# Three edits of order in a two-layer gated cross-attention kernel: when the router spreads its scores, when heads are transposed, when integers are transposed

## The chip, the cores and the metric

The kernel runs on one core of one Trainium2 chip. The metric is the device time in microseconds (us) of one execution; the median of several runs is compared. The core's engines run side by side, each through its own queue in order: TensorE (PE in the profile, with its weight loads as PEld), VectorE (DVE), ScalarE (ACT), GpSimd (POOL), and SyncE (SP), which here only issues transfers.

## The reference

Two layers act on x, which is 2 batches of 2048 tokens by 512 numbers. Each layer is a cross-attention to a context of 128 tokens and a feed-forward part, both gated:

```python
x = x + tanh(g_xattn[0]) * L0_xattn(layernorm(x), ctx_768, ...)
x = x + tanh(g_ffn[0])   * L0_ffn(layernorm(x), ...)
x = x + tanh(g_xattn[1]) * L1_xattn(layernorm(x), ctx_768, ...)
x = x + tanh(g_ffn[1])   * L1_ffn(layernorm(x), ...)
```

`L0_xattn` has 16 heads of 32 numbers, `L1_xattn` 16 heads of 64. `L0_ffn` is a mixture of depths: it works on 256 chosen tokens of each batch and leaves the others as they are.

```python
scores = x @ w_router
_, idx = top_k(scores, 256)
x_sel = take_along_axis(x, idx)
...                                   # causal self-attention and a gated MLP on x_sel
out = x.at[idx].set(x_proc)
```

`L1_ffn` multiplies by weights of -1, 0 and 1 with inputs rounded to integers in -128 to 127 (one scale per token), convolves over three neighbouring tokens, applies silu, rounds again and multiplies again.

## The kernel before

**Tiling.** Tokens go in 32 tiles of 128 rows; four tiles make a block of 512 tokens, four blocks a batch, so eight blocks in all, numbered 0 to 7. Matmuls in the attentions are in float32.

**Stages.** The first attention with the router (about 30 to 560 us of the profiled execution), the selected tokens' attention and MLP (560 to 830), the second attention with the first half of the integer feed-forward part beside it (830 to 1640), and the second half of that part (1640 to the end).

**Units.** `cross_attention` (L213) is called once for each layer. Its main loop (L338) steps through units: unit U is head u = U mod 16 of block n = U div 16. A unit issues, in this order:

- `scores` (L263) for the heads that share a tile of queries (four heads at once in the first layer, two in the second), and for its own head `probabilities` (L280): the softmax of `softmax_rows` (L113), which is a maximum `nmx` on DVE, four exps on ACT, a reciprocal `rden` on DVE, and the scaling of the tile A on POOL;
- at u == `ahead` (8 in the first layer, 10 in the second), `front` (L229) of the next block: layer norm on DVE, transposes `ptr` on PE, copies on ACT; and every fourth unit the next `queries` (projection `pq` on PE);
- `transposed` (L286) for the head two units back: four transposes `tp` on PE and a DVE copy to AT;
- `values` (L292), once in four units, for four heads of which the last is four units back: matmuls `po` on PE and ACT copies to OT;
- one step of `back` (L307), the output projection `pp` of an earlier block, which has eight steps and ends in a DVE addition to `x`;
- `beside(u)`, which advances other work.

A lies in a ring of four tiles, AT in a ring of six. In PSUM, `tp`, `po`, the router's `pb` and the gather's `pi` share two buffers (tag `o`).

**The router.** When `back` of block n ends, `router(n)` (L442) is appended to a list. `beside` (L436) takes two pieces of the list per unit. The pieces of a router are: the statistics; four rows (one for each tile: normalise on DVE, write it out through SP, multiply by `w_router` and sum with `ws` on DVE, scale `x` on ACT, write it out through SP); and then the work of `ranks` (L483). That begins with `spread` (L497), in which four transposes `pb` on PE broadcast the block's 512 scores over all partitions and an ACT copy puts them in `sb`. After it come counts on DVE (`junk`, L492, and `jd`, L514), which count for each token how many of its batch have a larger score: four tiles are new in each block, and the 4 x blk older ones of the batch are counted against the new scores, so the work grows with the block's number blk in its batch. After the last block of a batch, `gather` (L531) turns ranks to indices with 16 one-hot tiles `oh` on DVE and 32 small matmuls `pi` on PE, and two indirect transfers from POOL fetch the chosen rows.

With `back` of block n starting at unit 16n+19 and ending at 16n+26, the pieces start at unit 16n+26, and the spread comes in unit 16n+28, the same as the last row.

**The integers.** In the second attention, `quantize_rows` (L957) is a generator in a list `stream`, of which `beside4` takes two pieces per unit, and later one piece per third of an output tile. Its pieces are statistics, four tiles of scaling and maximum, four tiles of rounding to integers `xi` (ACT and then DVE, L980), then four steps of transposes `pt` on PE with an ACT copy to `xiT` each (L986 and L987), and the broadcast `inv_b`. The generator `first_half` of the same block follows in the same list; its matmuls `ph` (L1002) read `xiT`.

**Order.** The code's order gives each instruction its place, but an engine's queue in the trace isn't in that order word for word: instructions of different pieces are interleaved when the program is built. It is fixed from then on, and each engine waits for the instruction at its head.

Of the kernel before, what the change touches and what calls it, by code (L numbers as in the profile page):

```python
# [10 lines left out]
F32 = mybir.dt.float32  # L11
# [32 lines left out]
def flamingo_kernel(ctx: ExitStack, tc: tile.TileContext, a: dict, out: bass.AP):  # L44
# [167 lines left out]

    def cross_attention(  # L213
        W, act, hold, ps_mm, ps_sc, ps_o, row, xnT_bufs, ahead, rows_of, after_block, beside,
        after_units=lambda: None,
    ):

        L, nE, bias = W.L, W.nE, W.bias
        E = nE * P
        dh = E // H
        hpc = P // dh
        cpg = 4 // hpc
        scale = 1.0 / math.sqrt(dh)

        def front(n):  # L229

            tiles, xn, residual = rows_of(n)
            mv, rstd = ln_stats(tiles, L + "ln")
            for i, t in enumerate(tiles):
                normalize(xn[i], t, mv, rstd, i)
            xnT = act.tile([P, DC, BLK], F32, name="xnT", tag="xnT", bufs=xnT_bufs)
            transpose_block(
                ps_mm, "mm", xn, lambda d, pt: nc.scalar.copy(xnT[:, d, :], pt)  # L237
            )
            return residual, xnT

        def queries(xnT, grp):

            qT = [act.tile([P, BLK], F32, name="qT", tag="qT", bufs=3) for _ in range(cpg)]
            for c in range(cpg):
                e = grp * cpg + c
                pq = ps_mm.tile([P, BLK], F32, name="pq", tag="mm")
                for d in range(DC):
                    nc.tensor.matmul(  # L248
                        pq,
                        W.wq[:, d, ts(e, P)],  # L250
                        xnT[:, d, :],
                        start=(d == 0),
                        stop=(d == DC - 1),
                    )
                if bias:
                    nc.vector.tensor_scalar(
                        qT[c], pq, W.bq[:, e : e + 1], scale, ALU.add, ALU.mult
                    )
                else:
                    nc.scalar.activation(qT[c], pq, AF.Copy, scale=scale)  # L260
            return qT

        def scores(b, qT, e):  # L263

            sc = [ps_sc.tile([P, TB, M], F32, name="sc", tag="sc") for _ in range(hpc)]
            for t in range(TB):
                for h in range(hpc):
                    r = slice(h * dh, (h + 1) * dh)  # L270
                    nc.tensor.matmul(  # L271
                        sc[h][:, t, :],
                        qT[e % cpg][r, ts(t, P)],
                        W.kT[r, b, e, :],
                        start=True,
                        stop=True,
                    )
            return sc

        def probabilities(sc):  # L280

            A = act.tile([P, TB, M], F32, name="A", tag="A", bufs=4)
            softmax_rows(sc, TB, M, act, row, A)
            return A

        def transposed(A, AT):  # L286
            tp = ps_o.tile([P, TB, P], F32, name="tp", tag="o")
            for t in range(TB):
                nc.tensor.transpose(tp[:, t, :], A[:, t, :], ident)  # L289
            nc.vector.tensor_copy(AT, tp.rearrange("p t n -> p (t n)"))  # L290

        def values(b, AT, OT, grp):  # L292
            for c in range(cpg):
                po = ps_o.tile([P, BLK], F32, name="po", tag="o")
                for h in range(hpc):
                    hd = grp * 4 + c * hpc + h
                    nc.tensor.matmul(  # L297
                        po[h * dh : (h + 1) * dh, :],
                        W.v[:, b, ts(hd, dh)],
                        AT[c * hpc + h],  # L300
                        start=True,
                        stop=True,
                    )
                OT.append(hold.tile([P, BLK], F32, name="OT", tag="OT", bufs=nE + cpg))
                nc.scalar.copy(OT[-1], po)  # L305

        def back(n, residual, OT):  # L307

            tiles = residual()
            for t in tiles:  # L310
                nc.gpsimd.tensor_tensor(t, t, W.bo, ALU.add)  # L311
            for i, t in enumerate(tiles):
                pp = ps_mm.tile([P, D], F32, name="pp", tag="mm")
                for e in range(nE):
                    nc.tensor.matmul(  # L315
                        pp,
                        OT[e][:, ts(i, P)],
                        W.wo[:, e, :],
                        start=(e == 0),
                        stop=(e == nE - 1),  # L320
                    )
                    if e == nE // 2 - 1:
                        yield
                nc.vector.scalar_tensor_tensor(t, pp, W.g, t, ALU.mult, ALU.add)  # L324
                if i == TB - 1:
                    after_block(n, tiles)
                yield

        N = B * NBLK
        residual, xnT = {}, {}
        residual[0], xnT[0] = front(0)
        next_qT = queries(xnT[0], 0)
        As, AT, OT, out_of = {}, {}, {}, iter(())
        for U in range(N * H + 12):  # L338
            n, u = divmod(U, H)
            if n < N:  # L340
                grp, t = divmod(u, 4)
                if t == 0:
                    qT = next_qT
                if u % hpc == 0:
                    sc = scores(n // NBLK, qT, u // hpc)
                As[U] = probabilities(sc[u % hpc])
                if u == ahead and n + 1 < N:
                    residual[n + 1], xnT[n + 1] = front(n + 1)
                if t == 1 and grp < 3:
                    next_qT = queries(xnT[n], grp + 1)  # L350
                elif t == 1 and n + 1 < N:
                    next_qT = queries(xnT[n + 1], 0)
            V = U - 2
            if 0 <= V < N * H:
                AT[V] = act.tile([P, BLK], F32, name="AT", tag="AT", bufs=6)
                transposed(As.pop(V), AT[V])
            V = U - 4
            if 0 <= V < N * H and V % 4 == 3:
                n, grp = divmod(V // 4, 4)
                if grp == 0:  # L360
                    OT[n] = []
                values(n // NBLK, [AT.pop(i) for i in range(V - 3, V + 1)], OT[n], grp)
                if grp == 3:
                    out_of = back(n, residual.pop(n), OT.pop(n))
                    if n == N - 1:
                        after_units()
            next(out_of, None)
            beside(u)
# [23 lines left out]
    with ExitStack() as st:  # L392
# [49 lines left out]
        def router(n, tiles):  # L442
# [13 lines left out]
            for i in range(TB):  # L456
                t = t0 + i
                xn = act.tile([P, D], F32, name="xn2", tag="xn2", bufs=2)
                normalize(xn, x[t], mv, rstd, i)
                nc.sync.dma_start(out=xn_d[b][ts(t - b * TPB, P), :], in_=xn)  # L460
                ws = act.tile([P, D], F32, name="ws2", tag="ws2", bufs=1)
                nc.vector.scalar_tensor_tensor(
                    ws, xn, 1.0, w_router, ALU.mult, ALU.mult,
                    accum_out=score[:, t : t + 1],
                )
                nc.scalar.activation(
                    x[t],
                    x[t],
                    AF.Identity,
                    scale=keep_mul[:, i : i + 1],  # L470
                    bias=keep_add[:, i : i + 1],
                )
                nc.sync.dma_start(out=x_d[b][ts(t - b * TPB, P), :], in_=x[t])
                yield
            for work in ranks(b, blk):
                work()
                yield
# [102 lines left out]
        def stage1_rows(n):  # L580
# [3 lines left out]

        cross_attention(
            W0, act, act, ps_mm, ps_sc, ps_o, row, 2, 8, stage1_rows,
            lambda n, tiles: pending.append(router(n, tiles)), beside,
        )
        while pending:
            beside(None)  # L590
# [366 lines left out]
    def quantize_rows(g, tiles):  # L957
# [19 lines left out]
        for i, o in enumerate(tiles):  # L977
            nc.scalar.activation(o, o, AF.Copy, scale=s[:, i : i + 1], bias=RND)
            q = act4.tile([P, D], BF16, name="xi4", tag="xi4", bufs=TB)
            nc.vector.tensor_scalar(q, o, RND, 127.0, ALU.subtract, ALU.min)  # L980
            xi.append(q)
            yield
        for d in range(DC):
            pt = ps_mm.tile([P, BLK], BF16, name="pt4", tag="mm")
            for i, q in enumerate(xi):
# [373 lines left out]
```

## Time and profile before

| | us |
|---|---|
| median of 3 runs | 1854.61 (1854.43 to 1861.38) |
| the profiled execution | 1854.16 |
| its span, first to last instruction | 1852.5 |
| TensorE, weight loads, VectorE, ScalarE, GpSimd busy | 1660.6, 832.8, 1311.2, 1050.8, 527.4 |
| TensorE busy in 30 to 560 (first attention, router) | 440.2 of 530 |
| in 560 to 690 (selected attention) | 106.8 of 130 |
| in 690 to 880 (selected MLP, keys and values) | 181.3 of 190 |
| in 880 to 1640 (second attention) | 733.4 of 760 |
| in 1640 to the end (second half) | 182.7 of 213 |

Busy times overlap, since the engines work side by side. TensorE's granted clock is given as a share of full speed; its mean over the execution was 0.951. A line of the waits names the engine and line that stood, what it waited for, and the total, the number of times and the longest of these waits. In a timeline a line gives start, duration, engine, source line and operation, with the idle time before it in brackets.

### The profile page before, as it was taken

The numbers are of one execution on the slowest core, as the hardware profiler recorded it, in microseconds if no ns is written. First come the engines' busy times: TensorE is split into PE (matmuls) and PEld (weight loads), VectorE is DVE, ScalarE is ACT, GpSimd is POOL, SyncE is SP. The second block draws the span as 40 slices with busy tenths as digits, with TensorE's granted clock in tenths as the row PEclk, the third lists the DMA queues.
The fourth block names the chain that finished last, engine by engine and source line by source line (L and its number), as shares of the span: only waits on it lengthen the run. The fifth ranks groups of instructions, "written<-read, shape, count | busy, mean of one in ns | idle before, by whom it ended". The sixth has DMA issues, their size and how long they took to land.

```text
span 1852.5 us, 24500 instructions
## 1 busy us (share of the span) xinstructions
PE 1660.6 (90%) x7706; PEld 832.8 (45%) x7706; DVE 1311.2 (71%) x2769; ACT 1050.8 (57%) x3065; POOL 527.4 (28%) x666
## 2 busy tenths in 40 slices
PE   6989988888836989989999999999999999898969
PEld 3544544444413444445544454444444454443423
DVE  5777897887783642224537779889888888876966
ACT  2745544354501535304537778878787787754556
POOL 4534434342300320032214333322423243220200
PEclk9999999899967889999999999999999999998989
DMA  7011011011144009330011233334133133155465
GB/s 287 1 46 47 1 47 46 12 46 47 46 139 156 1 9 314 112 91 23 26 35 55 97 114 105 128 120 154 52 135 127 77 109 123 74 203 205 150 229 191
DMA packets 98456, 184.36 MB, mean 100 GB/s; under 512 B 11327, under 2 KB 30527, under 8 KB 94614
## 3 DMA queue, kind: packets, MB, share of 16 engines
q1 hardware_dynamic: 97430, 180.70, 28.1%
q0 software_dynamic: 896, 2.10, 0.6%
q8 instruction: 61, 1.00, 0.2%
q14 instruction: 69, 0.57, 0.1%
HBM read 108.31 MB, written 74.45 MB: 99 GB/s over the span
## 4 chain that ended last, share of the span: by engine, by line
PE 34%; DVE 14%; DMA 6%; ACT 5%; issue 2%; POOL 2%; SPq 1%; POOLq 0%; DVEq 0%; ACTq 0%
PE pp L315 8%; PE pq L248 7%; DVE h L1018 3%; PE ph L1002 3%; PE sc L271 2%; PE po L297 2%; PE pu L875 2%; PE pw L875 2%; PE acc L861 2%; PE tp L289 2%; PE po L1231 1%; DMA hf<-h_d 1%; DMA x<-h_d 1%; DVE u L1012 1%; DMA hq<-hq_d 1%
## 5 line engine op out<-in xcount | busy, mean ns | idle before, releaser
L119 ACT ACTIVATE A<-sc,nmx 128x128 f32<-128x128 f32 x1024 | 362.9, 377 | 171.7 <-DVE nmx L116 149.8
L128 POOL TENSOR_TENSOR A<-A,rden 128x512 f32<-128x512 f32 x256 | 274.4, 1073 | 479.9 <-DVE rden L127 373.1
L315 PE MATMUL pp<-L_wo,OT 128*128 128x512 f32 x768 | 365.9, 610 | 12.7 <-DVE x L324 4.7
L248 PE MATMUL pq<-xnT,L_wq 128*128 128x512 f32 x768 | 358.0, 612 | 0.2 <-ACT xnT L237 0.2
L119 ACT ACTIVATION_READ_ACCUMULATOR A<-sc,nmx 128x1 f32 x1024 | 221.4, 216 | 0.0
L248 PEld LDWEIGHTS pq<-xnT,L_wq 128*128 128x128 f32 x768 | 145.7, 197 | 159.6 <-issue 151.7
L116 DVE TENSOR_REDUCE nmx<-sc 128x4 f32<-128x512 f32 x256 | 169.2, 678 | 66.6 <-PE sc L271 66.5
L290 DVE COPY AT<-tp 128x512 f32<-128x512 f32 x256 | 172.8, 677 | 55.5 <-PE tp L289 55.1
L315 PEld LDWEIGHTS pp<-L_wo,OT 128*128 128x128 f32 x768 | 139.0, 195 | 159.6 <-issue 134.9
L1018 DVE SCALAR_TENSOR_TENSOR h<-u,cw,h 128x512 f32<-128x512 f32 x256 | 191.4, 782 | 5.6 <-ACT h L1014 5.1
L289 PE MATMUL tp<-ident,A 128*128 128x128 f32 x1024 | 164.3, 282 | 28.7 <-POOL A L128 26.6
L271 PE MATMUL sc<-L_kT,qT 32*128 32x128 f32 (+1 forms) x2048 | 164.0, 291 | 8.1 <-ACT A L119 5.1
L271 PEld LDWEIGHTS sc<-L_kT,qT 32*128 32x128 f32 (+1 forms) x2048 | 130.8, 189 | 87.2 <-issue 59.3
L289 PEld LDWEIGHTS tp<-ident,A 128*128 128x128 f32 x1024 | 119.3, 143 | 103.9 <-issue 48.0
L1231 PE MATMUL po<-w2q,hq 128*128 128x512 bf16 x512 | 121.2, 392 | 18.2 <-DVE hq L1213 8.5
L1014 ACT ACTIVATE h<-u,cb,cw 128x512 f32<-128x512 f32 x128 | 99.2, 809 | 64.7 <-DVE u L1012 60.1
L1002 PE MATMUL ph<-xiT,w1q 128*128 128x512 bf16 x512 | 125.1, 381 | 2.6 <-DVE u L1012 2.3
L297 PE MATMUL po<-AT,L_v 128*32 128x512 f32 (+1 forms) x512 | 115.9, 623 | 7.9 <-DVE AT L290 7.5
L305 ACT COPY OT<-po 128x512 f32<-128x512 f32 x96 | 55.7, 588 | 101.4 <-PE po L297 100.9
L1012 DVE TENSOR_TENSOR u<-ph,inv_b 128x512 f32<-128x512 f32 x128 | 85.1, 683 | 31.8 <-PE ph L1002 26.9
L1011 POOL COPY u<-carry 128x2 f32<-128x2 f32 x128 | 49.2, 386 | 192.0 <-DVE h L1018 159.6
L311 POOL TENSOR_TENSOR x<-x,L_bo 128x512 f32<-128x512 f32 x64 | 87.3, 1382 | 33.8 <-DMA x<-x_d 14.3
(216 smaller groups left out, 2203.3 us busy)
## 6 DMA issues: line engine op xcount, KB each, us to landing
h_d<-h SPq DMA_DIRECT2D x28, 1024.0 KB, 3.9
x_d<-x SPq DMA_DIRECT2D x64, 256.0 KB, 2.5
hf<-h_d SPq DMA_DIRECT2D x64, 256.0 KB, 3.3
x<-x_d SPq DMA_DIRECT2D x61, 256.0 KB, 4.5
x<-h_d SPq DMA_DIRECT2D x48, 256.0 KB, 5.7
x<-in_x SPq DMA_DIRECT2D x32, 256.0 KB, 5.4
xn_d<-xn SPq DMA_DIRECT2D x32, 256.0 KB
xf<-x_d SPq DMA_DIRECT2D x32, 256.0 KB, 3.8
```

Source lines behind the costliest of these rows:

```text
L116: nc.vector.tensor_reduce(nmx, sc, AX.X, ALU.max, negate=True)
L119: nc.scalar.activation(out_tile[:, h, :], sc[:, h, :], AF.Exp, bias=nmx[:, h : h + 1], accum_out=den[:, h : h + 1],)
L128: nc.gpsimd.tensor_tensor(out_tile, out_tile, rden.unsqueeze(2).to_broadcast([P, n, width]), ALU.mult,)
L248: nc.tensor.matmul(pq, W.wq[:, d, ts(e, P)], xnT[:, d, :], start=(d == 0), stop=(d == DC - 1),)
L271: nc.tensor.matmul(sc[h][:, t, :], qT[e % cpg][r, ts(t, P)], W.kT[r, b, e, :], start=True, stop=True,)
L289: nc.tensor.transpose(tp[:, t, :], A[:, t, :], ident)
L290: nc.vector.tensor_copy(AT, tp.rearrange("p t n -> p (t n)"))
L297: nc.tensor.matmul(po[h * dh : (h + 1) * dh, :], W.v[:, b, ts(hd, dh)], AT[c * hpc + h], start=True, stop=True,)
L315: nc.tensor.matmul(pp, OT[e][:, ts(i, P)], W.wo[:, e, :], start=(e == 0), stop=(e == nE - 1),)
L1002: nc.tensor.matmul(ph, w1q[:, d, ts(c, P)], xiT[g][:, d, :], start=(d == 0), stop=(d == DC - 1),)
L1018: nc.vector.scalar_tensor_tensor(z, u[:, ds(k, BLK)], cw[:, c, k : k + 1], z, ALU.mult, ALU.add)
L1231: nc.tensor.matmul(po, rows(c), w2q[:, c, :], start=(c == 0), stop=(c == HC - 1))
```

## The change

Three edits, none of which adds or removes a computation.

- `cross_attention` gets a parameter `lag`, 2 by default and 3 in the call for the first layer. `transposed` acts on the head `lag` units back in place of two, `values` and all that follows it on `lag` + 2 in place of four, the ring of A has `lag` + 2 tiles, and the loop runs `lag` + 10 units past the last head. So in the first layer A has five tiles, and `back`, with the router after it, comes one unit later.
- `router` yields six times more between the rows and `ranks`, except for the last block. At two pieces a unit the spread, the counts and the gather come three units further behind the rows (and, with `lag`, four units later than before: the spread in unit 16n+32).
- `quantize_rows` yields once more between the integers and their transposes, so that two pieces lie between the last integer and the first transpose's step in place of one.

```diff
     def cross_attention(
         W, act, hold, ps_mm, ps_sc, ps_o, row, xnT_bufs, ahead, rows_of, after_block, beside,
-        after_units=lambda: None,
+        after_units=lambda: None, lag=2,
     ):
...
-            A = act.tile([P, TB, M], F32, name="A", tag="A", bufs=4)
+            A = act.tile([P, TB, M], F32, name="A", tag="A", bufs=lag + 2)
             softmax_rows(sc, TB, M, act, row, A)
...
-        for U in range(N * H + 12):
+        for U in range(N * H + lag + 10):
...
-            V = U - 2
+            V = U - lag
             if 0 <= V < N * H:
                 AT[V] = act.tile([P, BLK], F32, name="AT", tag="AT", bufs=6)
                 transposed(As.pop(V), AT[V])
-            V = U - 4
+            V = U - lag - 2
             if 0 <= V < N * H and V % 4 == 3:
...
                 nc.sync.dma_start(out=x_d[b][ts(t - b * TPB, P), :], in_=x[t])
                 yield
+
+            for _ in range(6 if n + 1 < B * NBLK else 0):
+                yield
             for work in ranks(b, blk):
                 work()
                 yield
...
-            lambda n, tiles: pending.append(router(n, tiles)), beside,
+            lambda n, tiles: pending.append(router(n, tiles)), beside, lag=3,
         )
...
             xi.append(q)
             yield
+        yield
         for d in range(DC):
             pt = ps_mm.tile([P, BLK], BF16, name="pt4", tag="mm")
```

## The prediction

> **What bounds the kernel now.** I read the page first, then the waits of TensorE inside the first attention, its timeline around one of them, VectorE's timeline there, and a table of stretches.
>
> ```profile
> span 1852.5 us, 24500 instructions
> ...
> PE 1660.6 (90%) x7706; PEld 832.8 (45%) x7706; DVE 1311.2 (71%) x2769; ACT 1050.8 (57%) x3065; POOL 527.4 (28%) x666
> ...
> PE   6989988888836989989999999999999999898969
> ```
>
> TensorE is busy nine tenths of the span, least in the first third: the first attention with its router (about 30 to 560 us). A microsecond of its idle time there is one of the kernel's unless VectorE is the limit. What it waits for between 50 and 505 us (columns: total us, times, longest):
>
> ```profile
> PE pb L78 <- DVE ws L462: 21.2, 13, 2.5
> PE tp L289 <- POOL A L128: 17.0, 23, 2.2
> PE sc L271 <- ACT A L119: 3.0, 5, 1.3
> ```
>
> The first line is the router's spread: transposes `pb` that need the scores which `ws` has just written. One of its seven places, TensorE's timeline:
>
> ```profile
> 172.34 0.66 PE L289 MATMUL tp<-ident,A 128*128 128x128 f32 x4
> 175.45 0.45 PE L78 MATMUL pb<-ident,score 128*128 128x128 f32 x1 [2.45 <-DVE ws L462]
> 176.43 0.47 PE L78 MATMUL pb<-ident,score 128*128 128x128 f32 x1 [0.53 <-DVE ws L462]
> 176.69 5.33 PE L248 MATMUL pq<-xnT,L_wq 128*128 128x512 f32 x6
> 181.82 0.42 PE L78 MATMUL pb<-ident,score 128*128 128x128 f32 x1
> ```
>
> and VectorE's, which releases it:
>
> ```profile
> 173.42 0.23 DVE L450 TENSOR_SCALAR keep_mul<-ln_rstd,gate 128x4 f32<-128x4 f32 x1 [1.06 <-POOL ln_rstd L87]
> ...
> 180.04 0.66 DVE L462 SCALAR_TENSOR_TENSOR ws<-xn,w_router 128x512 f32<-128x512 f32 x1
> ```
>
> TensorE stands 2.98 us for two rows' scores although the projection `pq` behind them is ready; the rows last until 180.7. The four `pb` are not adjacent as in the code: the built program merges pieces by their place in the code and by what its order takes to be ready, and put the first two ahead of `pq`. The six `pq` then take 5.33 us; at 119.35, after the same stall, six take 2.74. The table of stretches says why (after the times: stretch, then PE, PEld, DVE, ACT, POOL busy; then clock, DMA share, GB/s):
>
> ```profile
> 173.00:175.60 2.60, 0.15 (x1) 0.18 (x1) 2.18 (x8) 0.86 (x2) 1.68 (x2) 0.95 0.25 95
> 175.60:182.50 6.90, 6.37 (x10) 2.67 (x11) 5.11 (x13) 4.75 (x17) 2.95 (x2) 0.52 0.73 271
> ...
> 118.20:125.10 6.90, 6.06 (x22) 2.95 (x22) 6.90 (x16) 5.75 (x21) 2.95 (x2) 1.00 0.76 284
> ```
>
> For 6.9 us after the stall the clock is 0.52. The same table cut at the spreads, one row per block of 16 heads:
>
> ```profile
> 118.20:175.40 57.20, 51.70 (x308) 27.40 (x308) 46.77 (x122) 30.85 (x142) 24.91 (x22) 1.00 0.10 38
> 175.40:236.90 61.50, 55.62 (x308) 29.87 (x309) 50.09 (x132) 31.22 (x142) 24.89 (x22) 0.94 0.10 35
> 236.90:302.00 65.10, 56.12 (x309) 29.78 (x309) 55.32 (x140) 31.18 (x142) 24.98 (x22) 0.95 0.09 34
> 302.00:380.20 78.20, 67.59 (x340) 37.48 (x340) 66.58 (x169) 31.56 (x142) 27.43 (x25) 0.87 0.10 34
> 380.20:439.80 59.60, 54.42 (x309) 28.66 (x310) 44.00 (x113) 31.14 (x143) 23.64 (x21) 0.94 0.10 37
> 439.80:496.20 56.40, 49.85 (x292) 26.39 (x293) 45.31 (x119) 28.89 (x138) 17.77 (x17) 1.00 0.10 38
> ```
>
> TensorE leads in most rows; in the third and fourth VectorE (55.3 of 65.1, 66.6 of 78.2) is close to being the limit, because rank counting grows with the block. In the second attention one line matters, waits from 880 to 1640 us:
>
> ```profile
> PE pt L986 <- DVE xi L980: 6.9, 10, 1.6
> ```
>
> [...] The trace agrees on the factor (5.33 against 2.74 us) and shows that a 2.98 us stall can be enough and that one of 3.13 us (at 115.8) was not: it is chance per stall. [...]
>
> **The spread moved.** It now follows its last row by six pieces, three units of about 57/16 = 3.6 us, so 11 us by code. Moved are, in each of seven blocks, four `pb`, the 0.58 us ACT copy `sb`, and all counting behind it on DVE (`junk`, `jd`); in the first block of a batch a POOL memset; for batch 0 also the gather: 16 `oh` on DVE, 32 `pi` on PE, two indirect DMAs on POOL. None goes through SP; the rows' SP writes stay before the pause. The two POOL DMAs (about 1 us each) pass some scalings of A, and their rows are read only at 565.7. The last block has no pause.
>
> (a) Idle removed. The seven stalls are the 21.2 us. The `pq` (ten instructions at once, 4.3 us) and two groups of ready `tp` (0.6 each) can fill them. Late next are the scores of the next four heads: they need exps that DVE's rows delay. ACT did exps at 177.07, 178.5 to 179.1, 180.2 to 181.1 and only at 184.08 the last of that pair, behind `sb`; without `sb` they end near 181.5, and scores, which restarted at 184.90, can start then: 3.4 of the 6.4 us that stall and slow clock cost are safe, the rest depends on DVE. Of 21.2 I take 17.
>
> (b) Clock restored. Length times (1 minus clock) gives 3.7, 3.3 and 3.6 us for rows two, three and five; row four holds one such period too, about 3.4; the block from 496 us lost 1.7. Sum 15.7 us; I take 11.5. Bounds of (a) and (b) together: 0 to 36.9.
>
> (d) Bunching. DVE's load per unit is 0.6 (`nmx`) + 0.6 (`AT`) + 0.1 (`rden`) + 0.3 (`qT`, `x`) = 1.6 us. From spread to next router start there were 14 units, now 11, in which DVE also has the next block's front (four statistics at 0.6, four normalisations at 0.5: 4.6 with the small ones) and rank work (`junk` and `jd` by the same stretches): 2.7+3.9 = 6.6, 10.4, 16.7, 22.0 us by block, with `oh` 5.9 more in the fourth. PE needs about 3.0 per unit (48 us of work a block). Eleven units: PE 33, DVE 22.2+16.7 = 38.9 for block three, 50 for block four; fourteen: PE 42, DVE 43.7 and 55. The excess grows from 2 and 13 us to 6 and 17. Counting may slip into DVE's gaps, so I take 6 of 8 lost (0 to 15). The gather's two `pi` hold both PSUM buffers that `tp` and `po` use, 345 to 357.7 before; it now comes one unit after the next block's statistics.
>
> (e) The end. Block 6's counting, 15 us of DVE, moves later, behind the last heads. There the chain is DVE: at 521.4 `pp` waited 4.7 us for an `x` that stood behind just this counting. Now `x` may come first. I take 0, from -6 to +8.
>
> **Lag 3 in the first attention.** The same transposes, one unit (3.6 us) later; A's ring grows to five, so no new wait for buffers; AT keeps its distance to `values`. 17.0 us of `tp` waiting for the scaling of A, longest 2.2, could all go by slack; but many follow DVE bursts that remain, and behind them PE meets the same late softmax as a wait of `sc`. I take 5 (0 to 12). Rows and back shift by a unit with their SP writes, which nothing reads soon.
>
> **Integer transposes.** One piece (half a unit, about 2 us in the second attention, a third of a tile later on) before `pt`; the 16 `pt`, four ACT copies and `inv_b`, and with them the hidden half and its SP writes, shift alike. 6.9 us of waits, plus 1.2 after 1640: longest 1.6, so a piece covers most, but first in line then is often `tp` or `po`. I take 3, from 8 gained to 4 lost if the last blocks' writes and reads come late.
>
> **Sum.** 17 + 11.5 + 5 + 3 - 6 = 30.5 us. The profiled execution took 1854.16 (span 1852.5 and 1.7 around it): 1823.7. It lies 0.45 under the median of 1854.61, so 1824.
>
> **Rivals.**
> - *Half comes back* (0.20): PE arrives earlier but meets DVE's rows: (a) and (b) keep the 3.4 us in seven blocks, 24, bunching takes 12, the rest nothing: 1842. For it: VectorE's 55 and 67 us in rows three and four. Against: in the other rows it has 10 or more us to spare.
> - *All of it goes* (0.08): 36.9 + 12 + 5 - 6 = 48: 1806 or less. Against: rows three and four can't go far below DVE's 55 and 67.
> - *No change in the order* (0.08): the built order still puts `pb` ahead of `pq`, since it goes by readiness as well as place: only lag and integers act, 1848 to 1856. Against: PE has ready work at all seven places, so the later place should decide.
> - *Rank work too late* (0.09, slower): one mechanism, counting pushed onto the next burst. The batch-0 gather then holds both buffers for DVE's backlog, another 15 us with 3 to 7 of half clock; block 6's counting falls wholly into the closing chain, 15; and the stalls return as waits of `sc` and `tp` on DVE, leaving 15 of (a) and (b). +15 + 5 + 15 - 15 = +20: 1874. It decides once the extra DVE delay exceeds about 31 us against what the stalls return. For it: DVE at 20.00 of 20 from 310 to 330. Against: DVE idles 4.45 us at 523 and in every light block.
>
> **How the numbers follow.** The forecast has 0.55 (1810 to 1836). Eight in ten reaches to most of the half-back case and the upper end of (a), (b) and lag, and takes in part of the unchanged order: 1800 to 1850, with 0.19 left out. 0.5% is about what can be told from no change (1845 to 1864): faster 0.79, same 0.12, slower 0.09.
>
> **What would show it.** Right: `pb` waiting under 3 us from 50 to 505, clock 1.00 behind each spread, block rows near 53, 55, 59, 72, 53, 52 us, `tp` waiting for A about 10, `pt` under 4. Wrong: `sc` or `tp` waits growing by what `pb` loses; a gather that holds its buffers longer than 12.7 us; the first stage's last count ending less than 15 us earlier than 559.9.

## The result and the profile after

The changed kernel takes 1901.09 us (median of 6 runs, 1900.28 to 1915.51), the kernel before 1855.02 beside it (1853.55 to 1861.38): ratio 1.0257, 95% interval 1.0225 to 1.0289. It is 46 us slower; 31 us faster was forecast. The page of the profiled execution:

```profile
span 1902.2 us, 24496 instructions
...
PE 1678.7 (88%) x7706; PEld 839.3 (44%) x7706; DVE 1329.0 (70%) x2769; ACT 1050.5 (55%) x3065; POOL 524.0 (28%) x666
...
PE   6988897899954989989999989999998999888968
```

The work is the same (7706 matmuls), yet TensorE is busy 18 us longer: more of them ran at half clock, where six `pq` took 5.33 us against 2.74 at full clock in the kernel before. The span grew by 49.7 us, by stage: the first, up to the last transpose `pb` of the last spread, 24.9 (it starts at 564.5 instead of 539.6); the selected tokens up to the last `kT` copy, -3.2 (busy time at half clock fell there from 28.3 to 20.7 us); from there to the last `tp`, 14.3; the rest, 13.7.

The waits of TensorE from 50 to 505 us in the kernel after (total, times, longest):

```profile
PE pp L315 <- DVE qT L256: 14.2, 5, 4.7
PE sc L271 <- DVE qT L256: 13.7, 8, 2.4
PE ptr L110 <- ACT xnT L237: 12.4, 7, 3.8
PE tp L289 <- ACT OT L305: 4.9, 5, 1.0
PE tp L289 <- DVE AT L290: 3.6, 7, 1.2
```

`pb` (21.2 us before) and `tp` waiting for A (17.0) are gone, as forecast. Others stand in their place. The stall that answers to the one shown of before, TensorE's timeline of the kernel after:

```profile
182.03 3.70 PE L248 MATMUL pq<-xnT,L_wq 128*128 128x512 f32 x8
185.71 0.63 PE L289 MATMUL tp<-ident,A 128*128 128x128 f32 x4
187.33 0.63 PE L289 MATMUL tp<-ident,A 128*128 128x128 f32 x4 [0.99 <-ACT OT L305]
190.39 1.22 PE L271 MATMUL sc<-L_kT,qT 32*128 32x128 f32 x8 [2.43 <-DVE qT L256]
191.54 1.11 PE L289 MATMUL tp<-ident,A 128*128 128x128 f32 x4
...
195.64 1.92 PE L297 MATMUL po<-AT,L_v 128*32 128x512 f32 x2
...
201.35 1.12 PE L78 MATMUL pb<-ident,score 128*128 128x128 f32 x4
202.26 3.77 PE L248 MATMUL pq<-xnT,L_wq 128*128 128x512 f32 x8
```

and VectorE's, which releases it:

```profile
187.24 0.66 DVE L462 SCALAR_TENSOR_TENSOR ws<-xn,w_router 128x512 f32<-128x512 f32 x1
...
187.82 1.25 DVE L101 TENSOR_SCALAR xn<-x,ln_mv,ln_rstd 128x512 f32<-128x512 f32 x1
189.00 0.68 DVE L116 TENSOR_REDUCE nmx<-sc 128x4 f32<-128x512 f32 x1
189.60 0.73 DVE L256 TENSOR_SCALAR qT<-pq,L_bq 128x512 f32<-128x512 f32 x1
```

`pq` now runs at once, during the rows and not behind them; its bias addition `qT` stands in VectorE's queue behind the same rows (the last `pq` ended at 185.7, `qT` starts at 189.60), and the scores stand for it. So TensorE stands as long as before, and what it finds behind the stall is no longer ten ready `pq`, but scores, transposes and `po` in turn. Four such stretches in the columns of the prediction's table (PE, PEld, DVE, ACT, POOL busy; clock; DMA share, GB/s):

```profile
124.10:137.80 13.70, 11.95 (x53) 7.28 (x54) 9.28 (x19) 6.82 (x32) 5.59 (x6) 0.50 0.16 58
188.90:202.60 13.70, 12.21 (x53) 7.54 (x54) 9.02 (x19) 6.65 (x32) 5.43 (x5) 0.50 0.14 54
257.20:270.90 13.70, 12.07 (x53) 7.40 (x54) 9.16 (x19) 6.70 (x32) 5.48 (x6) 0.50 0.16 59
332.30:346.00 13.70, 13.68 (x48) 7.61 (x49) 8.83 (x22) 6.97 (x35) 5.35 (x6) 0.50 0.03 11
```

After the stall the clock stays at half for 13.7 us, though TensorE is busy for 12 to 13.7 of them; behind the stall shown of before it was 6.8. The next table adds this up for every whole kernel that was run: the first stage from 40 us to the start of its last `pb`; TensorE's idle time in it; its busy time while the granted clock was half (worked out from the records of the clock and the matmuls); and the whole time at half clock from 40 to 495 us, which the expectations below call half-clock time. Busy time at half clock is counted as costing half of itself (5.33 us against 2.74 for the six `pq` above). A ratio is taken against runs of the kernel before on the same chip, whose medians were 1854.7 to 1857.0.

The four last columns are of one profiled execution of each kernel, and that lay up to 11 us off the median (e5 10.9, e3 8.8 and e4 6.9 below it, e13 7.6 above), so small differences in them prove nothing. The large ones stand in the mean granted clock of all timed executions too: 0.950 in the kernel before, 0.934 after, 0.9385 in e4, 0.940 in e13, and 0.950 again in e18.

| kernel | median, us | ratio to before (95%) | stage 1 | idle | busy at half | half-clock time |
|---|---|---|---|---|---|---|
| before | 1855.02 | | 499.6 | 67.3 | 48.5 | 41.0 |
| after | 1901.09 | 1.0257 (1.0225 to 1.0289) | 524.5 | 72.5 | 100.0 | 104.6 |
| e1_pause | 1866.77 | 1.0057 (1.0032 to 1.0082) | 509.1 | 69.9 | 94.1 | 85.3 |
| e2_lag | 1869.30 | 1.0070 (1.0052 to 1.0087) | 515.2 | 62.1 | 91.3 | 88.7 |
| e3_ints | 1884.62 | 1.0166 (1.0128 to 1.0205) | 498.7 | 68.9 | 41.6 | 34.1 |
| e4_pause_lag | 1879.73 | 1.0133 (1.0098 to 1.0168) | 526.0 | 72.4 | 102.9 | 105.8 |
| e5_ints_abs | 1875.84 | 1.0099 (1.0071 to 1.0126) | 501.8 | 66.7 | 54.0 | 51.2 |
| e6_lag_tp | 1857.69 | 1.0022 (0.9999 to 1.0045) | 499.7 | 65.0 | 59.6 | 51.2 |
| e7_rows | 1854.11 | 0.9977 (0.9963 to 0.9991) | 500.1 | 67.3 | 78.1 | 75.1 |
| e9_pause_lag_tp | 1862.50 | 1.0039 (1.0022 to 1.0055) | 503.9 | 70.5 | 78.7 | 71.7 |
| e10_rows_lag_tp | 1852.88 | 0.9980 (0.9965 to 0.9994) | 494.1 | 66.2 | 64.6 | 64.9 |
| e11_pause_lag_short | 1846.13 | 0.9946 (0.9921 to 0.9970) | 488.7 | 68.9 | 62.9 | 64.9 |
| e12_before_short | 1828.97 | 0.9848 (0.9820 to 0.9875) | 478.7 | 61.4 | 67.4 | 75.1 |
| e13_back | 1874.34 | 1.0090 (1.0073 to 1.0107) | 522.6 | 64.6 | 97.9 | 88.7 |
| e14_values | 1874.60 | 1.0110 (1.0093 to 1.0127) | 515.8 | 67.3 | 83.7 | 75.1 |
| e15_front | 1862.91 | 1.0046 (1.0028 to 1.0064) | 507.9 | 70.5 | 62.5 | 61.4 |
| e16_front_pause_lag | 1872.57 | 1.0082 (1.0059 to 1.0105) | 518.8 | 68.4 | 99.6 | 99.0 |
| e17_back_queries | 1875.85 | 1.0107 (1.0090 to 1.0124) | 517.8 | 90.2 | 68.5 | 68.3 |
| e18_pause_lag_queries | 1848.84 | 0.9956 (0.9939 to 0.9972) | 496.2 | 73.9 | 61.2 | 58.0 |

For the change: half clock (100.0 - 48.5) / 2 = 25.8 us, idle 5.2, and 6.1 less in what is left of the busy time, together the 24.9. That rest, busy time reduced to full clock, differs by up to 17 us between the kernels with the full rows, mostly at the scores and the values, and goes with how the queue cuts them up. In the kernel before, 32 scores in one go take as long as 8 between other work:

```profile
84.06 1.17 PE L271 MATMUL sc<-L_kT,qT 32*128 32x128 f32 x32
130.19 1.15 PE L271 MATMUL sc<-L_kT,qT 32*128 32x128 f32 x8
```

The same 992 scores stand in 75 runs in the kernel before, in 56 after and in 37 in e18, and take 65.3, 50.3 and 46.4 us of this rest; the values take 33.2, 45.0 and 39.9. The count of runs isn't all of it (54.8 us in 73 runs in e7); a score's own duration in the profile, 0.27 us in the median, says little where 32 stand within 1.17 us; and what decides the cutting was not tried.

The two later stages belong to the integers: without the later transposes, in e4, they took 809.8 and 221.4 us, in the kernel after 828.1 and 235.9 (before 813.9 and 222.2). Waits from 880 to 1640 us, after (of before, `pt` 6.9, `tp` for A 5.8, `po` for AT 5.2):

```profile
PE tp L289 <- POOL A L128: 9.8, 6, 2.9
PE po L297 <- DVE AT L290: 4.9, 7, 1.8
PE po L297 <- ACT OT L305: 3.0, 6, 1.2
PE tp L289 <- DVE AT L290: 2.9, 2, 1.5
PE ptr L110 <- ACT xnT L237: 2.6, 1, 2.6
PE pt L990 <- DVE xi L983: 2.3, 5, 0.6
```

`pt` lost 4.6 us of waiting as forecast; the other five lines gained 12, and idle time from the last `kT` to the last `tp` went from 35.2 to 48.4 us.

### The profile page after: what moved, and what is told of

The parts are those of the page before. It is cut to its first block, busy times and chain, and to the rows that moved or that the text cites. A ratio compares the mean times of both kernels' runs of the same rounds, so it can differ in the third digit from the quotient of the medians.

```text
span 1902.2 us, 24496 instructions
## 1 busy us (share of the span) xinstructions
PE 1678.7 (88%) x7706; PEld 839.3 (44%) x7706; DVE 1329.0 (70%) x2769; ACT 1050.5 (55%) x3065; POOL 524.0 (28%) x666
## 5 line engine op out<-in xcount | busy, mean ns | idle before, releaser
L248 PE MATMUL pq<-xnT,L_wq 128*128 128x512 f32 x768 | 352.9, 608 | 2.7 <-ACT xiT L991 1.6
L290 DVE COPY AT<-tp 128x512 f32<-128x512 f32 x256 | 172.3, 676 | 68.0 <-PE tp L289 67.4
L289 PE MATMUL tp<-ident,A 128*128 128x128 f32 x1024 | 167.7, 290 | 31.7 <-POOL A L128 12.6
L1022 DVE SCALAR_TENSOR_TENSOR h<-u,cw,h 128x512 f32<-128x512 f32 x256 | 185.6, 761 | 3.1 <-ACT h L1018 2.2
L271 PE MATMUL sc<-L_kT,qT 32*128 32x128 f32 (+1 forms) x2048 | 160.1, 302 | 19.8 <-DVE qT L256 16.3
L297 PE MATMUL po<-AT,L_v 128*32 128x512 f32 (+1 forms) x512 | 137.3, 676 | 11.3 <-DVE AT L290 8.2
L495 DVE TENSOR_SCALAR_CACHE_REDUCE junk<-sb,score 128x512 bf16<-128x512 f32 (+14 forms) x102 | 80.7, 831 | 15.2 <-ACT sb L507 15.2
```

Of the source, the lines that this page charges most:

```text
L248: nc.tensor.matmul(pq, W.wq[:, d, ts(e, P)], xnT[:, d, :], start=(d == 0), stop=(d == DC - 1),)
L271: nc.tensor.matmul(sc[h][:, t, :], qT[e % cpg][r, ts(t, P)], W.kT[r, b, e, :], start=True, stop=True,)
L297: nc.tensor.matmul(po[h * dh : (h + 1) * dh, :], W.v[:, b, ts(hd, dh)], AT[c * hpc + h], start=True, stop=True,)
L1022: nc.vector.scalar_tensor_tensor(z, u[:, ds(k, BLK)], cw[:, c, k : k + 1], z, ALU.mult, ALU.add)
```

## The experiments

**One edit at a time.** e1 has the pause alone, e2 lag 3 alone, e3 the later integer transposes alone, e4 the first two.

```diff
# e1, e4
+            for _ in range(6 if n + 1 < B * NBLK else 0):
+                yield
# e2, e4
-            V = U - 2
+            V = U - lag
-            V = U - 4
+            V = U - lag - 2
# e3
             xi.append(q)
             yield
+        yield
```

> Only the pause of six pieces before the spread; lag 2, integers as before. Theory A (the lag does the harm in the first stage: it moves the router's rows one unit against the four-unit beat of queries, so that qT stands behind the rows on DVE): the stalls at pb are gone, qT is copied before the rows end, first stage 10 to 30 us shorter, 1825 to 1845 in all. Theory B (the pause does it: once pb is out of the way TensorE runs into DVE's rows with nothing left): last pb near 560, first stage +20 to +25, 1875 to 1885.

> Only lag 3 in the first attention; no pause, integers as before. Theory A: first stage longer by 15 to 30 us with waits of sc and pp on qT, 1870 to 1885. Theory B: the pb stalls stay as before, waits of tp for A fall from 17 to a few us, first stage within 10 us of before, 1845 to 1860.

> Only the extra yield before the integers' transposes. Theory C (this yield costs the 28 us that the second attention and the second half lost together): first stage and selected stage as before to 1 us, end at 1875 to 1885. Rival D (the order of the later stages changed only because the program as built is another one everywhere, the yield itself is worth a few us): 1848 to 1860.

> Pause and lag, integers as before: first stage as in the changed kernel (last pb at 564). Theory C: second attention and second half as before, 1870 to 1877 in all. Rival D: they lose here too, 1885 to 1900.

Each edit is slower alone: the pause by 0.57%, the lag by 0.70%, the integers by 1.66%. Pause and lag together cost 24.5 us (1879.73 against 1855.21 in that set), about their sum. The pause moves the stall to the transposes (`tp` waiting for A 29.7 us, up to 4.1 a time) and doubles the busy time at half clock; the lag has less idle time than before, 62.1 us, and is slower through the clock alone.

What e3 loses at the end is one chain. Timeline of e3, SyncE, ScalarE, VectorE, TensorE:

```profile
1696.21 5.44 SPq L1050 DMA_DIRECT2D h_d<-h  x1
...
1712.35 1.91 ACT L1051 ACTIVATE h<-h 128x2048 f32<-128x2048 f32 x1 [8.90 <-DMA h_d<-h]
1714.17 1.32 ACT L978 ACTIVATE x<-x,xqs 128x512 f32<-128x512 f32 x2
1715.43 0.42 DVE L980 TENSOR_SCALAR xi<-x 128x512 bf16<-128x512 f32 x1
...
1715.91 0.50 PE L987 MATMUL pt<-identb,xi 128*128 128x128 bf16 x3 [9.23 <-DVE xi L980]
```

The same in the kernel before:

```profile
1684.90 0.38 SPq L1049 DMA_DIRECT2D h_d<-h  x1
1692.51 1.91 ACT L1050 ACTIVATE h<-h 128x2048 f32<-128x2048 f32 x1 [2.10 <-DMA h_d<-h]
...
1699.73 0.34 PE L986 MATMUL pt<-identb,xi 128*128 128x128 bf16 x3 [1.21 <-DVE xi L980]
```

One piece later, the write of the hidden half is issued 11.3 us later; its issue takes 5.44 us instead of 0.38, and the write 16.1 us instead of 7.6 from its issue to the start of the Abs. That Abs works in place, so it may not start before the write has read `h`; behind it in ScalarE's queue is the rounding of the last rows, behind that `xi`, and TensorE stands 9.23 us (8.9 at the same `pt` in the kernel after). e5 lets the Abs write elsewhere in that one place:

```diff
-                nc.scalar.activation(h, h, AF.Abs)
+                z = h
+                if g == LAST - 1 and k == HC // GC - 1:
+                    h = hidden(act4, name="h", tag="h", bufs=3)
+                nc.scalar.activation(h, z, AF.Abs)
```

> As e3_ints (one more piece before the integer transposes), but for the last hidden group of group 6 the Abs of ScalarE writes into another buffer of `h` instead of in place, so that it no longer waits for the write of `h` to memory. Theory (that write, issued late on SyncE behind the loads of the last blocks, holds ScalarE's in-order queue with the rounding of the last rows behind it): TensorE's wait of 9.2 us for `xi` in the last stage falls to about 1.5, the last stage (end of the second attention to the end) goes from 236.9 us back to 222 to 228, and the time is about 1870, since the second attention's +7.7 us stay. Rival (the stage is longer because the transposes themselves are late, whatever the write does): last stage 234 or more, time about 1885.

The rest after the last `tp` took 218.5 us (236.9 in e3, 222.2 before), `pt` waited 0.5 in it, and the time came to 1875.84 us, ratio 1.0099 instead of 1.0166, where 1870 was expected. So the write held ScalarE. The second attention did not recover (826.5 us against 821.6 in e3 and 813.9 before). What makes the waits there grow was not tried apart and stays open.

**Where the stall goes.** e6 lags the transposes of A alone, while values, back projection and router keep their units; e7 is the kernel before with a piece more behind every row, so that the rows come one per unit; e9 and e10 add e6's edit to the pause and to e7.

```diff
# e6, e9, e10: V = U - lag for transposed, V = U - 4 kept for values
-            V = U - 2
+            V = U - lag
# e7, e10: inside the loop over the four rows
+                if n + 1 < B * NBLK:
+                    yield
```

> Lag 3 for the transposes of A alone; values, back projection and router keep their units. Theory of phase (lag 3 costs because back, router rows and values move by one unit against the queries and scores of every fourth unit, so that late scores are followed by narrow matmuls and not by the wide query projection): half-clock time in the first stage about 40 us as in the kernel before, last spread at 540 us or earlier, 1850 or a little less. Rival (the later transposes cost by themselves): half-clock time 80 us or more, last spread near 555, about 1869.

> The kernel before with one more piece after each row of the router (none in the last block), so that the rows are spread over twice as many units; nothing else moved. Theory (the burst of four rows on VectorE is what makes scores, transposes or spreads late wherever they stand): the spread's waits fall from 21.2 us to under 8 without new waits for `qT` or `A` growing by as much, half-clock time 40 us or less, time 1830 to 1852. Rival (VectorE's sum over the block is the limit, not the burst, and counting that comes later runs into the next front): waits for `qT`, `A` or `xnT` of 15 us or more, half-clock time 70 us or more, 1858 to 1885.

> The six-piece pause before the spread together with lag 3 for the transposes of A alone (queries, values, back projection and router keep their units). Theory (with the pause alone the stall only moved to the transposes that wait for POOL's scaling of A, because two or three row operations of ScalarE and VectorE lie inside that softmax; and lag 3 as the change makes it costs by shifting the router rows against the queries): the wait of `tp` for A falls from 29.7 us to under 8, the spread's wait stays near 0, half-clock time in the first stage 60 us or less, last spread before 540 us, time 1830 to 1852. Rival (the next in line, the scores that need `qT` or the query's `xnT`, are late by the same row operations, so the stall moves once more): waits of `sc` for `qT` or A of 15 us or more in place of those of `tp`, half-clock time 75 us or more, 1858 to 1875.

> One router row per unit (as e7_rows) together with lag 3 for the transposes of A alone. Theory: the wait of `tp` for A, 31.2 us with the spread-out rows alone, falls to under 8, half-clock time in the first stage from 75 to 50 us or less, time 1825 to 1845, faster than both kernels. Rival (the stall moves to the next operand of the same late softmax, `sc` or `po`): waits of `sc` for A or `qT` and of `po` for `AT` grow by what `tp` loses, half-clock time stays at 70 us or more, time 1850 to 1862 as with the rows alone.

Lag for the transposes alone does next to nothing (1.0022). It takes the wait for A out of e9 and e10 completely, and idle time stays: in e9 `tp` waits for AT 18.1, `ptr` for `xnT` 9.1, `sc` for `qT` 7.9; in e10 `sc` waits for `rden` 11.0 and `tp` for AT 10.5. Idle time lies between 62 and 74 us in every kernel of the table with the full rows but e17. The rival of e9 held; e7 and e10 gain 0.2%, with the rival's waits.

**The clock by itself.** e8b runs stretches of one kind of matmul behind an idle gap:

```python
for kind, n in ((full, 24), (narrow_rows, 72), (turned, 36), (narrow_columns, 36), (mixed, 50), ...):
    for i in range(n):
        kind(i, gap)      # mixed: scores' shape (narrow_rows) and transposes (turned) in turn
    ...
    idle()                # 16 dependent DVE operations
```

> Leaves out the whole computation: only stretches of matmuls of one kind each behind an idle gap of some 10 us of TensorE, to measure the clock: full 128x128 by 512 columns; four 32-row pieces by 512 columns (the shape of the scores); four 128x128 transposes; four pieces with 32 output columns; scores and transposes in turn; each twice. Theory (after a gap the granted clock comes back by how much of the array works, not by busy time alone): the full kind is back at 1.00 within about 7 us, the 32-row, transposing and mixed kinds stay near 0.5 for 13 us or longer. Rival (busy time alone counts): all kinds are back at 1.00 after the same 4 to 7 us.

The theory fell for the pure kinds: the clock was back 3.6 us (full), 3.3 and 3.5 (32 rows), 3.7 and 3.9 (transposes), 5.1 and 5.2 us (32 columns) after the first matmul. For scores and transposes in turn it took 17.9 us the first time and 4.3 the second, with the same instructions and no wait. Both stretches, at half and after (PE, PEld, DVE, POOL busy; clock):

```profile
129.70:147.60 17.90, 17.86 (x120) 12.32 (x120) 0.00 (x0) 0.00 (x0) 0.50 0.00 1
147.60:163.00 15.40, 15.39 (x181) 10.97 (x180) 0.58 (x1) 0.00 (x0) 1.00 0.01 1
297.00:301.30 4.30, 4.30 (x33) 2.96 (x33) 0.00 (x0) 0.00 (x0) 0.51 0.00 0
301.30:324.40 23.10, 23.07 (x272) 16.48 (x268) 0.59 (x1) 0.00 (x0) 1.00 0.01 1
```

So an unbroken run of that mixture stayed at half for 17.9 us once, and for 4.3 us the other time.

The records of the kernels' traces add what single stretches can't show. In these records the clock changed only on a grid of steps of 3.413 us, and what TensorE did in one step went with the clock of the next. The first stages of the 19 kernels (from 45 us to the last `pb`) hold 2329 steps at full clock. All 133 of them with less than 1.3 us of busy time were followed by half clock, but only 22 of the 1829 with 2.5 us or more. Of the 439 steps at half clock, only 1 of the 65 that were busy for less than 80% was followed by full clock. 332 were busy for 95% or more. Full clock followed in 116 of the 117 of these in which three or more wide projections (`pq` or `pp`, 128 rows by 512 columns) started, in 49 of 61 with one or two, and in 33 of 154 with none. So in these stages the way back hardly ever came without busy time (1 of 65), 134 of the 332 busiest steps stayed at half too, and what the matmuls were went with it. This is a count over kernels and not an experiment, but e17 and e18 below test it.

**Are the rows the cause?** e11 (made from e4) and e12 (from the kernel before) cut the router's rows short, so that other tokens are chosen than in the reference:

```diff
-                normalize(xn, x[t], mv, rstd, i)
-                nc.sync.dma_start(out=xn_d[b][ts(t - b * TPB, P), :], in_=xn)
+                nc.sync.dma_start(out=xn_d[b][ts(t - b * TPB, P), :], in_=x[t])
...
-                    ws, xn, 1.0, w_router, ALU.mult, ALU.mult,
+                    ws[:, 0:64], x[t][:, 0:64], 1.0, w_router[:, 0:64], ALU.mult, ALU.mult,
...
-                nc.scalar.activation(x[t], x[t], AF.Identity, ...)
```

> As e4_pause_lag (the pause and lag 3, no later integer transposes), but the router's rows are cut short: no normalisation, no scaling of the residual on ScalarE, and scores from 64 of 512 columns of the unnormalised residual, so that a row takes some 0.2 us of VectorE instead of 1.2 and none of the 0.8 us of ScalarE. Everything else, pieces, writes and ranking, stays. Theory (the rows' burst on VectorE and ScalarE makes TensorE stand about 2.7 us once per block wherever the spread and the transposes are put, and moving these only changes who stands first and how long the clock stays at half): with the burst gone no stall over 1.5 us recurs with the rows, half-clock time in the first stage is below 50 us instead of 105.8, and the time lies within 6 us of e12_before_short. Rival (pause and lag cost by themselves, by the place of the shifted work against the queries): 12 us or more above e12_before_short.

> The kernel before with the router's rows cut short in the same way (no normalisation, no scaling of the residual, scores from 64 columns). Theory: the spread's wait of 21.2 us falls under 5, half-clock time in the first stage under 30 us, last spread at 525 us or earlier, time 1825 to 1842. Rival (the stall has another cause, such as the next block's normalisation on VectorE): a stall of 2 us or more per block remains with other operands named, last spread 532 or later, time 1845 or more.

What is cut of the rows is worth 27 us to the kernel before, and its `pb` wait goes. But a stall of 2.6 us per block stays (`tp` for AT, 14.9 us in all, behind the next block's normalisation), `tp` waits longer for A (25.3 us instead of 17.0), and busy time at half clock grows to 67.4 us; the gain in the first stage is mostly at the scores (45.0 us instead of 65.3, reduced to full clock). Pause and lag still cost 17.2 us on top (1846.13 against 1828.97). The theory that the rows explain everything fell; its rival, the place of the shifted work, held.

**Which shifted work?** e13 starts the back projection, and so the router, one unit later; e14 the values too; e15 moves the next block's front four units earlier; e16 does that to e4.

```diff
# e13
-                    out_of = back(n, residual.pop(n), OT.pop(n))
+                    held = back(n, residual.pop(n), OT.pop(n))
...
             next(out_of, None)
+            if held is not None:
+                out_of, held = held, None
# e14
-            V = U - 4
+            V = U - 4 - later
# e15, e16
-            W0, act, act, ps_mm, ps_sc, ps_o, row, 2, 8, stage1_rows,
+            W0, act, act, ps_mm, ps_sc, ps_o, row, 2, 4, stage1_rows,
```

> The kernel before, but the back projection of the first attention and with it the router start one unit later; transposes and values keep their units. Theory (what lag 3 costs is the later back projection and rows, which then fall together with the next block's normalisation and its query projections): 1863 to 1872, half-clock time in the first stage 75 us or more. Rival (the cost is that values come in the same unit as the next scores): 1853 to 1859, half-clock time as in the kernel before, 41 us.

> The kernel before, but values one unit later in the first attention, and so back projection and router too; transposes of A keep their unit. If back and rows carry the cost (theory), this is within 4 us of e13_back, at 1863 to 1872; if the values in the same unit as the scores carry it (rival), 1863 to 1872 with e13_back at 1853 to 1859.

> The kernel before with one number changed: the next block's front (statistics, normalisation, transposes) in the first attention at the 4th instead of the 8th head of a block. Theory (the stall of about 2.5 us per block stands at the place where VectorE has the router's start, its rows and the next block's normalisation together): the spread's wait of 21.2 us falls under 8 with no other wait of `sc` or `tp` growing by as much, half-clock time 30 us or less, time 1825 to 1845. Rival (the front costs as much wherever it stands, there beside the back projection): stalls of 2 us or more at another place in each block, time 1850 to 1862.

> As e4_pause_lag (pause and lag 3, no later integer transposes), with the front at the 4th head. Theory (pause and lag cost because the shifted rows meet the next block's normalisation): within 6 us of e15_front. Rival (they cost by their own places): 12 us or more above e15_front, 1865 to 1882.

The later back projection and router alone cost 0.9%, with values 1.1%: this is what lag 3 costs, not the transposes. And e13 has less idle time than the kernel before (64.6 us; no wait of `pb` is over 1.41): its 23.0 us in the first stage are the clock, (97.9 - 48.5) / 2 = 24.7. One stretch of e13:

```profile
187.50:204.60 17.10, 16.91 (x61) 9.54 (x62) 14.38 (x40) 8.06 (x38) 4.92 (x5) 0.51 0.14 51
```

An earlier front doesn't help: in e15 the stalls stay where they were (`pb` 18.0 us), and e16 is 9.7 us above e15, between theory and rival. So the coincidence with the front is at most part of the cause: with the early front, pause and lag leave 99.6 us of busy time at half clock, hardly less than e4's 102.9.

**What stands behind the stall.** e17 (made from e13) and e18 (from e4) move the query projections by the same unit as the rest:

```diff
-                if t == 1 and grp < 3:
+                if t == lag - 1 and grp < 3:
...
-                elif t == 1 and n + 1 < N:
+                elif t == lag - 1 and n + 1 < N:
```

(e17: `1 + later` in place of `lag - 1`.)

> As e13_back (back projection and router one unit later), with the query projections of the first attention one unit later as well, so that they stand to the rows as in the kernel before. Theory (what follows the stall decides how long the clock stays at half: the wide query projection brings it back, scores and transposes in turn do not): busy time at half clock in the first stage falls from 97.9 us to 60 or less, time 1853 to 1862. Rival (the loss comes from the later rows themselves, or the queries now come too late for their scores): 80 us or more at half clock, 1868 or more.

> As e4_pause_lag (pause and lag 3, no later integer transposes), with the query projections one unit later. With the pause the stall stands in front of scores and transposes, not of the queries, so the theory expects only part of the 24 us back: 1862 to 1872, busy time at half clock 75 to 90 us instead of 102.9. Rival (place against the queries is all that matters): as the kernel before, 1850 to 1858. Rival 2 (it makes no difference): 1876 or more.

e18 beat its expectation and both kernels: 0.9956 (0.9939 to 0.9972). Its idle time is that of e4 (73.9 against 72.4 us); busy time at half clock is down from 102.9 to 61.2. TensorE's timeline at one stall of e18:

```profile
183.05 0.63 PE L289 MATMUL tp<-ident,A 128*128 128x128 f32 x4 [2.56 <-DVE AT L290]
183.51 4.42 PE L248 MATMUL pq<-xnT,L_wq 128*128 128x512 f32 x6
187.72 1.10 PE L289 MATMUL tp<-ident,A 128*128 128x128 f32 x8
```

The stall is as long as ever; the six `pq` are behind it again, and the clock is back at 187.9, after 3.4 us. e17 got its clock back (97.9 to 68.5 us), but idle time rose by 25.6 us (`pb` for AT 19.4, `tp` for A 19.7, `sc` for A 12.6), so its time didn't move: there the expectation failed. Order behind the stall is worth some 21 us, and it can be eaten up by waits of its own. It isn't all that e18 gained over e4 (30.9 us by the medians): some 10 us more are busy time reduced to full clock, in which the scores went from 50.4 to 46.4 us and the values from 45.0 to 39.9. And in the first stage e18 doesn't lead the kernel before by its clock or its idle time, which are both worse (61.2 against 48.5 us, 73.9 against 67.3), but by its scores, 46.4 us against 65.3.

## Why the prediction was wrong

**(a) Idle removed, 17 us.** This failed. `pb` did lose its 21.2 us, by the mechanism named: `pq` and ready `tp` fill the place. But idle time in the first stage rose from 67.3 to 72.5 us. The step took "late next are the scores" to be cured where ScalarE's exps end earlier; the trace has them late by VectorE, where `qT` stands behind the rows. e1, e9 and e10 show the stall at a new operand each time. It was the wait's name that went.

**(b) Clock restored, 11.5 us.** The term that failed most: 25.8 us lost instead. It took half clock to go with the stall. The stall stayed, and `pq`, which had stood behind it, had been sent ahead. The periods went to 13.7 us, and the blocks, forecast at 53, 55, 59, 72, 53 and 52 us, came out at 64.6, 68.4, 72.3, 76.4, 63.1 and 50.4 (cut at the end of each `pb`); e13 shows the same loss without more idle time, e18 most of it undone. That any busy stretch brings the clock back soon was the author's assumption, which the traces of before had not shown. The runs show it for one kind of matmul (3.3 to 5.2 us in e8b) and not always for scores and transposes in turn (17.9 us fully busy in e8b the first time, 4.3 the second; 17.1 in e13, where a few `pq`, `pb` and `po` stood among them). Nor was it chance alone whether a stall halves the clock, as the prediction had it: its stall of 2.98 us left one step of 3.413 us with 1.06 us of busy time, the one of 3.13 us lay across two, with 1.86 and 1.84 (of the steps between 1.3 and 2.5 us, 82 of 367 were followed by half clock). Why the mixture stayed at half once and the other time didn't was not settled.

**(d) Bunching, -6, and (e) the end, 0.** The fourth of these blocks takes 76.4 us with VectorE busy 67.4, where 78.2 and 66.6 stood: VectorE didn't become the limit. The end held: the last count closes at 584.8 instead of 559.9, the 24.9 us by which all of the stage is later.

**Lag 3, +5.** The wait for A went, as forecast, and e6 puts the worth of that at nothing (1.0022). The cost is in the half sentence on rows and back shifting by a unit, priced only by their writes: 17 to 20 us (e13, e14).

**Integers, +3, from 8 gained to 4 lost.** `pt` fell to 2.3 us from 880 to 1640, inside the forecast; the edit still lost 21 us (after against e4) to 29 (e3). The clause "if the last blocks' writes and reads come late" named the right place and was sized at 4: the `h_d` write alone cost 9.2 us at one wait (e3), and with its hold on ScalarE gone the time fell by some 9 us (e5).

**The rivals.** The side was that of "rank work too late", 1874, but not its mechanism: the gather held its buffers from 389.8 to 398.9 us, 9.1 against 12.7 before. Of its three parts only the last came, stalls returning as waits on DVE, and it was priced without the clock.

## What to carry to other kernels

Before a wait is priced as a gain, ask which instruction takes its place while the burst that made it is still there: here idle time stayed within 62 to 74 us over nearly all reorderings, and only its name changed. Price a stall of TensorE with what follows it: ready wide matmuls behind it brought the clock back in 3.4 to 6.8 us, stretches of mostly narrow ones left it at half for up to 17, so sending the ready work ahead of the stall can cost more than the stall (here 25.8 us at half clock, where the `pb` waits had been 21.2). When one step is moved, move what it meets as well, and try it: pause and lag were 1.3% slower with the queries in place and 0.4% faster with the queries moved along.

## What the runs showed of the hardware

In these traces the clock moved in steps of 3.413 us. In the 19 kernels' first stages it came back after nearly all steps that were busy for 95% or more and had three or more wide projections (116 of 117), and seldom after such busy steps without any (33 of 154). Two stretches of scores and transposes in turn, fully busy (e8b), came back to full clock after 17.9 and 4.3 us; they lay differently on the grid, and the first had five whole steps at half, the second one. With float32 transposes alone it was back in 3.7 and 3.9 us (e8b). And the clock fell without one long stall: in e13 waits of 0.65, 0.28 and 1.41 us in a row left one step with 1.14 us of busy time, and of the 133 steps at full clock with less than 1.3 us of busy time in the 19 kernels' first stages none kept full clock behind it.
